# An attention block with a gated branch on one core: first unit's last scores from split operands, second chunk's statistics a step later

## The chip, the cores and the metric

The kernel runs on one core of one Trainium2 chip. The core has five engines that run side by side and meet through semaphores: TensorE (PE, matmuls; PEld is its weight load), VectorE (DVE), ScalarE (ACT), GpSimd (POOL) and SyncE (SP, which here only issues DMAs). Each engine works off its own list of instructions in order. The metric is the device time of one execution in microseconds.

## What is computed

The input x is 2 batches of 1024 tokens with 512 features. All weights are float32.

```python
xn = layernorm(x)
q, k, v = xn @ Wq.T + bq, xn @ Wk.T + bk, xn @ Wv.T + bv      # 32 heads of 16
att = softmax(where(causal, q @ k.T / sqrt(16), -inf))        # per head
s = (att @ v) @ Wo.T + bo
base = xn @ W_base.T + b_base
route_w = top-2 of softmax(xn @ W_gate.T), renormalised       # 8 experts
delta = ((xn @ A.T) * route_w) @ B                            # rank 16 each
out = x + s * silu(base + delta)
```

## The kernel before

The tokens of a batch are two *chunks* of 512 (c = 0, 1). Heads go in four groups of eight (oc = 0 to 3). A *unit* is (batch, group, chunk of the queries); there are 16, and their order is (0,0,0), (0,1,0), (0,0,1), (0,1,1), (0,2,0), (0,3,0), (0,2,1), (0,3,1) and the same for batch 1. A unit is worked off in *steps*: 5 for chunk 0, 13 for chunk 1, so that `plan` has 144 steps, 0 to 143. Units 0, 1 and 2 have the steps 0 to 4, 5 to 9 and 10 to 22; unit 6, (0,2,1), begins at step 46.

A step does this. `scores(n)` multiplies keys and queries of eight heads into two PSUM banks (tiles s, two buffers of a pair's half each; line 1723). ACT takes the exponential of each bank into a tile pt. `values(n - 1)` multiplies the previous step's pt with the values into av (line 1775). `masked(n)` has POOL blank the upper triangle of pt (line 1751). Then `fill(n)` puts other work on PE until the step has its share: projections (`pq`, `pk`, `q`), values and gate products (`p`), the route product (`ph`, of the experts' weights), the output product (`po`). All of it goes through `matmul` (line 258) into PSUM tiles of the tag mm, which has two buffers: each product can begin when the reader of the last but one is through.

Scores come in two forms. The first unit multiplies plain float32: the queries are laid out in two copies, each masked to one head of a pair (`queries(par)` in `first_task`, two DVE operations), and the keys are kf. All other units have *split* operands: a rounded part and the remainder, in tiles of a reduced float format (F32R), so that a score is two cheaper products (`halves`). To make them, ACT copies the rounded part (`split_keys`, `split_queries`), DVE subtracts it, ACT copies the remainder of the queries (`copy_remainder`), and SP moves rows between partitions with DMAs (`place_keys`, `place_queries`, two DMAs each). In the kernel before, the first unit's keys are split too, by the function `apart` at step 4 or later, since unit 2 uses them; its queries are not.

The values of the first chunk are made by a seven-product scheme for 2x2 blocks, which needs sums of weights (t1 to t4, from wv) and of tokens (asum, named s[0] to s[3], from xnT). For the first chunk DVE makes them in `early_values`; the products are named p1, p2, p6, p7, p4 there and p5, p3 in `early_rest`, and `early_add` adds each into v.

The second chunk of batch 0 is normalised in `layernorm_task`: four tiles of statistics (`bn_stats`), the power on POOL (line 282), four normalisations, and then twice: four transposes of 32x32 blocks into the tile sq, one store of sq to memory (scr), four reads of scr into xnT. The tile sq has one buffer (`bufs=1`).

Who comes when is settled when the program is built: `fill` keeps lists (`later`, `urgent`, `splits`, `turns`) and `Task` objects with due times, and a reckoning of when DVE and ACT are free (`Metered`, line 56, through which every DVE and ACT operation is recorded, so that they all show line 56; SP's DMAs show line 72). What it settles is a fixed list for each engine. `room` counts free buffers of a tag. At the end, `test_task` tests that the softmax's sums are in range (tiles ok and fine), and `post_tile` normalises the last unit's tiles (rc_last, olast).

Of the kernel before, what the change touches and what calls it, by code (L numbers as in the profile page):

```python
# [8 lines left out]
F32 = mybir.dt.float32  # L9
# [9 lines left out]
P = 128  # L19
# [12 lines left out]
NEG = -3.0e38  # L32
NF = 2 + 4 * 2 * 4
WARM = 10


Z_LOW, Z_HIGH = 1.0e-20, 1.0e20
# [60 lines left out]
def direct(ctx, tc, sound, x, wq, wk, wv, wo, wb, wa, wg, wB, bq, bk, bv, bo, bb, out):  # L98
# [148 lines left out]
    WAIT = object()  # L247
    PAUSE = object()
    turned_at, now = {}, [0]
    xns, xnTs, kTs, qTs, vs, gs, oTs, kfs = {}, {}, {}, {}, {}, {}, {}, []  # L250

    def mm_tile(name):
        return ps_mm.tile([P, D], F32, tag="mm", name=name)
# [42 lines left out]
    def layernorm_task(b, c):  # L296


        xt = chunk_tile(b, c)
        for i in range(NS):  # L300
            i0 = c * C + i * P
            sp.dma_start(
                out=xt[i * SQ : (i + 1) * SQ],
                in_=x[b, i0 : i0 + P].rearrange("(t r) d -> r t d", r=SQ),
            )
        if b == 0:
            load_rest()
        tiles = [xt[:, t] for t in range(TT)]
        for _ in range(3 if b else 1):
            yield WAIT  # L310
        s = yield from statistics(tiles, True)
        if b:
            yield WAIT
        for t in range(0, TT, 2):
            normalize(tiles[t : t + 2], s[0][:, t : t + 2], s[1][:, t : t + 2])
            yield PAUSE
        if b:
            yield WAIT
        xnT = sb.tile([P, KC, C], F32, tag="xnT", bufs=3, name=f"xnT_{b}_{c}")
        for k0 in range(0, KC, 2):  # L320
            sq = sb.tile([P, 2, NS, TT, SQ], F32, tag="sq", bufs=1, name="sq")
            for t in range(TT):
                yield PAUSE
                ve.transpose(
                    out=sq[:, :, :, t],
                    in_=tiles[t][:, k0 * P : (k0 + 2) * P].rearrange(
                        "p (k q d) -> p k q d", k=2, q=NS
                    ),
                )
            scr = dram.tile([NS, SQ, 2, NS, TT * SQ], F32, tag="scr", name="scr")  # L330

            def store(sq=sq, scr=scr, place=None):
                sp.dma_start(
                    out=scr.rearrange("i d k q m -> (i d) (k q m)"),
                    in_=sq.rearrange("p k q t r -> p (k q t r)"),
                )
                if place:
                    behind.append(place)
                    landed(place, now[0] + 3)

            def place(k0=k0, scr=scr):
                for q in range(NS):
                    sp.dma_start(
                        out=xnT[q * SQ : (q + 1) * SQ, k0 : k0 + 2].rearrange(
                            "d k (i m) -> d k i m", i=NS
                        ),
                        in_=scr[:, :, :, q].rearrange("i d k m -> d k i m"),
                    )
                if k0:
                    turned_at[b, c] = now[0] + int((sp.landing() - sp.now) / 3.4)  # L350

            if not b:
                store()
                place()
                yield WAIT
                continue
            later.append((now[0] + b, lambda s=store, p=place: s(place=p)))
            for _ in range(0 if k0 else 1 + b):
                yield WAIT
        xnTs[b, c] = xnT  # L360

    def first_task():
# [1 line left out]
        xnT = sb.tile([P, KC, C], F32, tag="xnT", bufs=3, name="xnT_0_0")  # L364
        qT = sb.tile([P, 2, C], F32, tag="qT", bufs=2, name="qT_0_0_0")
        kT = sb.tile([P, C], F32, tag="kf", bufs=2, name="kf_0_0_0")
        xnTs[0, 0], qTs[0, 0, 0] = xnT, qT
        kfs.append(kT)
        pq = ps_av.tile([P, C], F32, tag="av", name="pq_first")
        pk = ps_av.tile([P, C], F32, tag="av", name="pk_first")  # L370

# [20 lines left out]
        def queries(par):  # L392
            ve.tensor_scalar(
                qT[:, par], pq, bq_sb[:, 0:1], half[:, par : par + 1], ALU.add, ALU.mult
            )
# [29 lines left out]
        turn(3)  # L425
        room["x"] += 1
        project_first(pk, wqks[0][:, 3 * KC :], 2)
        project_first(pq, wqks[0][:, 2 * KC : 3 * KC], TT - 1)
        queries(0)
        queries(1)  # L430
        ve.stream_shuffle(b_pair, b_sb, PAIRED)
        ve.tensor_tensor(b_less, b_pair[:, 0:KC], b_pair[:, KC:], ALU.subtract)
        project_first(pk, wqks[0][:, 3 * KC :], 3)
        keys(1, TT)
        kTs[0, 0, 0] = sb.tile([P, 2, C], F32R, tag="kT", bufs=4, name="kT_0_0_0")
        low = sb.tile([P, C], F32, tag="rb", bufs=1, name="low_0_0_0")

        def apart():
            ve.stream_shuffle(low, kT, PAIRED)
            split_keys(kTs[0, 0, 0], low, low)  # L440
            later.append((now[0] + 1, lambda: place_keys(kTs[0, 0, 0], low)))

        later.append((0, lambda: pair_up(wqks[1])))
        paired = lambda: pair_up(wqks[0])
        costs[paired], costs[apart] = (1.1, 5), (1.1, 6)
        later.append((3, paired))
        later.append((4, apart))
        yield 8 * MM

    def qk_task(b, oc, c):  # L450
# [72 lines left out]
            both = qT[:, 2 * par : 2 * par + 2].bitcast(F32)  # L523
            sp.dma_start(out=both[1 - par :: 2], in_=both[par::2])

    def last_unit(unit):
        return 1 if unit == units[-1] else 0

    def split(b, oc, c, qf, kf):

        qT, kT = split_tiles(b, oc, c)
        split_keys(kT, kf, kf)

        def queries():
            split_queries(qT, qf)
            room["acc"] += 1
            later.append((now[0] + 1, remainder))

        def remainder():
            copy_remainder(qT)  # L540
            urgent.append((now[0], lambda: place_queries(qT)))

        by = starts[b, oc, c] - last_unit((b, oc, c))
        costs[queries], costs[remainder] = (1.1, by - 4), (0.6, by - 3)
        later.append((now[0] + 1, queries))
        urgent.append((now[0] + 1, lambda: place_keys(kT, kf)))
# [282 lines left out]

    def early_values():

        x0 = xnTs[0, 0]
        at = lambda i, j: x0[:, 2 * j : 2 * j + 2, BK * i : BK * i + BK]
        early_at["w"] = raw = {
            (i, j): wv_sb[:, 2 * i : 2 * i + 2, BK * j : BK * j + BK]
            for i in range(2) for j in range(2)
        }
        t = {  # L840
            n: sb.tile([P, 2, BK], F32, tag="wp", bufs=NWP, name=f"wt{n}") for n in range(1, 5)
        }
        early_sums.update({f"t{n}": t[n] for n in t})
        early_at["s"] = s = [
            sb.tile([P, 2, BK], F32, tag=f"sum{n}", bufs=1, name=f"asum{n}") for n in range(4)
        ]
        vt = value_tile(0, 0)
        for i in range(TT):
            vs[0, i] = vt[:, i]
        hv = heads(vt)  # L850
        early_at["v"] = slot = lambda i, j: hv[:, 2 * i : 2 * i + 2, H // 2 * j : H // 2 * (j + 1), 0:HD]
        s11, s12, s21, s22 = slot(0, 0), slot(0, 1), slot(1, 0), slot(1, 1)
        ve.tensor_tensor(t[1], raw[0, 1], raw[0, 0], ALU.subtract)
        ve.tensor_tensor(s[2], at(0, 0), at(1, 0), ALU.subtract)
        ve.tensor_tensor(s[1], at(1, 1), s[2], ALU.subtract)
        ve.tensor_tensor(t[2], raw[1, 1], t[1], ALU.subtract)
        ve.tensor_tensor(t[3], raw[1, 1], raw[0, 1], ALU.subtract)
        p1 = yield from early_product("p1", at(0, 0), raw[0, 0])
        early_add(s12, p1, early_bias(0))
        ve.tensor_tensor(t[4], raw[1, 0], t[2], ALU.subtract)  # L860
# [621 lines left out]
    for b in range(NB):  # L1482
        for c in range(NC):
            s0 = starts[b, 0, c]
            xn = [("xnT", b, c)]
            if not b and not c:
                room["x"] -= 1
                Task(1, first_task(), 8 * MM, takes={"xnT": 1, "qT": 1, "kT": 1}, uses=xn)
            else:
                Task(  # L1490
                    s0 - (12 if c else 25) if b else -9, layernorm_task(b, c), 0.0, after=s0 - (44 if c == 0 else 30) if b else -9,
                    takes={"x": 1, "xnT": 1}, frees={"x": 1},
                )
# [58 lines left out]
            else:  # L1552
# [2 lines left out]
                n = len(units) - 3  # L1555
                Task(len(plan) - 12, test_task(0, n, 0), 0.0, after=before - 10)
                Task(
                    len(plan) - 1, test_task(n, n + 2, 1), 0.0, after=len(plan) - 3,
                    ready=lambda: sum(len(x) for x in posts.values()) == len(units) - 1,
                )  # L1560
                for t in range(TT - 1):
# [48 lines left out]
    def fill(n):  # L1610
# [52 lines left out]
        enough = lambda more=0.65: late_by(n + 1, begins, more) > 0  # L1663
        calm = lambda more: act.free + more < begins + 0.75
        for x in [x for x in splits if x[0] <= n]:
            if room["qT"] and room["kT"] and (calm(1.1) or n >= starts[x[2]] - 5 - last_unit(x[2])):
                splits.remove(x)
                room["qT"] -= 1
                room["kT"] -= 1
                x[1]()  # L1670
# [38 lines left out]
    def scores(n):  # L1709
# [1 line left out]
        place_urgent(n)  # L1711
        ss = [ps_s.tile([P, 2, C], F32, tag="s", name=f"s{p}") for p in range(2)]
        for m, (par, kt, q0, w, col) in enumerate(pieces):
            first_unit = (b, oc, c) == units[0]
            halves = 1 if first_unit else 2
            keys = kfs[0] if first_unit else kTs[b, oc, kt // TT][:, par]
            q = qTs[b, oc, c]
            for half_ in range(halves):
                for s in range(4):
                    rows = slice(32 * s, 32 * s + 32)  # L1720


                    nc.tensor.matmul(  # L1723
                        ss[s // 2][:, s % 2, col : col + w],
                        lhsT=keys[rows, kt % TT * P : kt % TT * P + P],
                        rhs=q[rows, halves * par + half_, q0 : q0 + w],
                        start=m + half_ == 0,
                        stop=m == len(pieces) - 1 and half_ == halves - 1,
                    )
# [572 lines left out]
```

## Time and profile before

| | us |
|---|---|
| median of 3 timed runs | 544.42 (544.01 to 545.55) |
| the profiled execution, its own time | 544.48 |
| its span in the profile | 542.7 |
| PE busy | 531.8 |
| ACT busy | 351.6 |
| DVE busy | 340.9 |
| PE weight load busy | 282.7 |
| POOL busy | 116.1 |

The granted TensorE clock was 0.998 of full speed over the span. The DMA queue that SP feeds moved 76.78 MB and took 44.7% of the 16 DMA engines' time.

How to read the profile: a timeline line gives start and duration in us from the span's start, the engine, the source line, the operation and the tiles as out<-in, then the number of instructions that were merged into the line, and in brackets how long the engine stood idle before it and what ended that. Matmuls are pipelined and their ends are modelled, so two neighbouring PE groups overlap by some 0.1 to 0.2 us; the distance from start to start is what a group really takes from PE. In the list of waits, the columns are the total in us, how often, and the longest.

### The profile page before, as it was taken

The numbers are of one execution on the slowest core, as the hardware profiler recorded it, in microseconds if no ns is written. First come the engines' busy times: TensorE is split into PE (matmuls) and PEld (weight loads), VectorE is DVE, ScalarE is ACT, GpSimd is POOL, SyncE is SP. The second block draws the span as 40 slices with busy tenths as digits, with TensorE's granted clock in tenths as the row PEclk, the third lists the DMA queues.
The fourth block names the chain that finished last, engine by engine and source line by source line (L and its number), as shares of the span: only waits on it lengthen the run. The fifth ranks groups of instructions, "written<-read, shape, count | busy, mean of one in ns | idle before, by whom it ended". The sixth has DMA issues, their size and how long they took to land.

```text
span 542.7 us, 19905 instructions
## 1 busy us (share of the span) xinstructions
PE 531.8 (98%) x8623; PEld 282.7 (52%) x8623; DVE 340.9 (63%) x706; ACT 351.6 (65%) x387; POOL 116.1 (21%) x249
## 2 busy tenths in 40 slices
PE   7999999999999999999999999999999999999994
PEld 7546445544455554454645554454545564456672
DVE  4863586665585876476369766574277544749843
ACT  2457754776776876757667756657667776877630
POOL 2213401020033422030123320130113330121200
PEclk9999999999999999999999999999999999999999
DMA  7626356356526583813665545640124121653301
GB/s 251 159 93 219 132 165 223 100 187 208 158 100 226 184 265 118 236 43 100 191 164 199 178 142 167 196 153 24 63 95 144 61 85 44 236 170 91 99 29 61
DMA packets 67744, 78.15 MB, mean 144 GB/s; under 512 B 9928, under 2 KB 52944, under 8 KB 67136
## 3 DMA queue, kind: packets, MB, share of 16 engines
q1 hardware_dynamic: 67632, 76.78, 44.7%
q8 instruction: 70, 1.15, 0.9%
q14 instruction: 26, 0.21, 0.1%
q10 hardware_dynamic: 16, 0.00, 0.0%
HBM read 45.34 MB, written 19.37 MB: 119 GB/s over the span
## 4 chain that ended last, share of the span: by engine, by line
PE 94%; DVE 3%; DMA 2%; issue 0%; SPq 0%; DVEq 0%
PE av L1775 26%; PE p L258 25%; PE s L1723 18%; PE q L258 14%; PE ph L258 3%; PE po L258 2%; PE pk L258 1%; PE pq L258 1%; DMA wqk<-in_wq_dram 1%; PE pq_first L388 1%; PE h L258 1%; DMA kept<-w_gate 1%; DVE g L56 1%; PE pk_first L388 0%; PE pt_o L258 0%; DVE wt L56 0%
## 5 line engine op out<-in xcount | busy, mean ns | idle before, releaser
L56 ACT ACTIVATE pt<-s 128x1024 f32<-128x1024 f32 x288 | 290.5, 1024 | 151.0 <-PE s L1723 147.0
L1751 POOL TENSOR_SCALAR_AFFINE_SELECT pt<-pt 128x256 f32<-128x256 f32 (+1 forms) x224 | 107.4, 494 | 399.5 <-ACT pt L56 398.9
L1775 PE MATMUL av<-pt,v 128*32 128x512 f32 (+3 forms) x1680 | 154.3, 467 | 0.2 <-DVE oT L56 0.2
L1723 PE MATMUL s<-qT,kT 32*128 32x512 f32 (+3 forms) x1616 | 106.7, 363 | 0.0
L1723 PEld LDWEIGHTS s<-qT,kT 32*128 32x128 f32 x1616 | 61.2, 183 | 56.5 <-issue 34.6
L1775 PEld LDWEIGHTS av<-pt,v 128*32 128x32 f32 x1680 | 40.9, 108 | 53.6 <-issue 38.3
L258 PE MATMUL p<-wt,asum 128*32 128x256 f32 x960 | 58.4, 379 | 0.4 <-DVE v L56 0.4
L258 PE MATMUL q<-asum,wqk 128*32 128x256 f32 x832 | 51.1, 379 | 0.0
L258 PEld LDWEIGHTS p<-wt,asum 128*32 128x32 f32 x960 | 30.9, 110 | 30.0 <-issue 12.6
L258 PE MATMUL q<-xnT,wqk 128*32 128x256 f32 x624 | 39.5, 379 | 0.0
L258 PEld LDWEIGHTS q<-asum,wqk 128*32 128x32 f32 x832 | 26.8, 110 | 23.7 <-issue 6.6
L258 PEld LDWEIGHTS q<-xnT,wqk 128*32 128x32 f32 x624 | 20.2, 110 | 18.5 <-issue 6.6
L56 DVE SCALAR_TENSOR_TENSOR kf<-q,kf 128x256 f32<-128x256 f32 x39 | 16.5, 422 | 20.6 <-PE q L258 20.0
L56 DVE TENSOR_TENSOR g<-p,g 128x512 f32<-128x512 f32 x20 | 13.8, 689 | 23.5 <-PE p L258 23.4
L258 PE MATMUL p<-w,xnT 128*32 128x256 f32 x448 | 27.6, 379 | 0.0
L56 DVE TENSOR_TENSOR v<-p,v 128x512 f32<-128x512 f32 x22 | 14.9, 683 | 13.4 <-PE p L258 13.3
L258 PE MATMUL p<-w,asum 128*32 128x256 f32 x320 | 21.0, 379 | 0.0
L258 PEld LDWEIGHTS p<-w,xnT 128*32 128x32 f32 x448 | 14.8, 110 | 10.6 <-issue 3.3
L258 PEld LDWEIGHTS ph<-wag_sb,xnT 128*32 128x32 f32 x512 | 15.2, 110 | 3.9 <-issue 3.3
L56 DVE TENSOR_TENSOR x<-p,x 128x512 f32<-128x512 f32 x15 | 10.3, 685 | 10.4 <-PE p L258 10.4
L258 PE MATMUL ph<-wag_sb,xnT 128*32 128x136 f32 x512 | 16.6, 279 | 0.0
L56 ACT ACTIVATE qT<-qf 128x1024 fp32r<-128x1024 f32 x15 | 15.8, 1054 | 0.1
(156 smaller groups left out, 563.6 us busy)
## 6 DMA issues: line engine op xcount, KB each, us to landing
wt<-kept SPq DMA_DIRECT2D x36, 256.0 KB
qT<-qT SPq DMA_DIRECT2D x30, 256.0 KB
x<-in_x_dram SPq DMA_DIRECT2D x16, 256.0 KB
kept<-wqk SPq DMA_DIRECT2D x16, 256.0 KB
wqk<-kept SPq DMA_DIRECT2D x4, 1024.0 KB
kT<-kf SPq DMA_DIRECT2D x30, 128.0 KB
scr<-sq SPq DMA_DIRECT2D x6, 512.0 KB
xnT<-scr SPq DMA_DIRECT2D x24, 128.0 KB
```

The costliest lines, as they stand in the source:

```text
L56: return getattr(self.engine, name)(*args, **named)
L258: nc.tensor.matmul(o[j : j + 32], lhsT=lhsT[:, j : j + 32] if len(lhsT.shape) == 2 else lhsT[:, j // 32], rhs=rhs, start=start, stop=stop,)
L388: nc.tensor.matmul(ps[:, cols], lhsT=w[:, k, :], rhs=xnT[:, k, cols], start=k == 0, stop=k == KC - 1)
L1723: nc.tensor.matmul(ss[s // 2][:, s % 2, col : col + w], lhsT=keys[rows, kt % TT * P : kt % TT * P + P], rhs=q[rows, halves * par + half_, ...
L1751: nc.gpsimd.affine_select(out=d, in_=d, compare_op=ALU.is_ge, fill=0.0, base=0, pattern=[[0, d.shape[1]], [1, P]], channel_multiplier=-1,)
L1775: nc.tensor.matmul(avs_now[par][32 * s : 32 * s + 32, q0 : q0 + w], lhsT=vs[b, kt][:, h * VS - HD * par : h * VS - HD * par + HP], rhs=pt[ ...
```

## The change

Five things are done.

1. `early_begin`, called in `first_task` before the last part of the query projection, makes three weight sums (t1, t2, t3) and one token sum (s[2]); they were made in `early_values`, behind the queries. It calls the vector engine directly, so the planner's reckoning doesn't count them.
2. The first unit's queries are written by ACT as a whole too (qf). `apart` now comes in step 0 and splits keys and queries: two shuffles, two ACT copies, two differences, then the keys' DMAs and, by `remainder`, the copy of the remainder and the queries' DMAs. Steps below `SPLIT_FROM` (3) use the plain operands (`whole_first`), steps 3 and 4 the split ones; the plain queries' buffer is given back at step 2.
3. The second chunk's `layernorm_task` waits two turns instead of one ahead of its statistics (batch 0).
4. `last_unit` becomes `sooner`, which is 1 for unit 6 also: its split may be a step earlier.
5. The second range test may begin at step `len(plan) - 4` (140) instead of 141.

In the lists that result, PE has the same order of work as before, with the split form in steps 3 and 4. On DVE, the second chunk's normalisations and all eight transposes come behind the difference of unit 1's keys and ahead of the additions of p5; before, the normalisations and the first four transposes came ahead of p4's addition, and the second four behind unit 1's keys. On SP, the first unit's four split DMAs come ahead of unit 1's, and the first store and reads of scr, which came ahead of unit 1's queries and keys, come behind them; the first unit's keys came behind den before. On POOL, the power comes behind step 2's masks. Around step 45, unit 6's query split stands one step earlier on ACT, DVE and SP.

```diff
+SPLIT_FROM = 3
...
-        for _ in range(3 if b else 1):
+        for _ in range(3 if b else 2):
             yield WAIT
...
-        xnTs[0, 0], qTs[0, 0, 0] = xnT, qT
-        kfs.append(kT)
+        xnTs[0, 0] = xnT
+        whole_first.extend((qT, kT))
...
         project_first(pk, wqks[0][:, 3 * KC :], 2)
+        early_begin()
         project_first(pq, wqks[0][:, 2 * KC : 3 * KC], TT - 1)
         queries(0)
         queries(1)
+        qf = sb.tile([P, C], F32, tag="qf", bufs=2, name="qf_0_0_0")
+        act.activation(qf, pq, AF.Identity, bias=bq_sb[:, 0:1])
...
-        kTs[0, 0, 0] = sb.tile([P, 2, C], F32R, tag="kT", bufs=4, name="kT_0_0_0")
+        q2, k2 = split_tiles(0, 0, 0)
         low = sb.tile([P, C], F32, tag="rb", bufs=1, name="low_0_0_0")
+        turns.append((SPLIT_FROM - 1, lambda: room.update(qT=room["qT"] + 1)))
 
         def apart():
+            qs = sb.tile([P, C], F32, tag="qf", bufs=2, name="qs_0_0_0")
             ve.stream_shuffle(low, kT, PAIRED)
-            split_keys(kTs[0, 0, 0], low, low)
-            later.append((now[0] + 1, lambda: place_keys(kTs[0, 0, 0], low)))
+            ve.stream_shuffle(qs, qf, PAIRED)
+            split_keys(k2, low, low)
+            split_queries(q2, qs)
+            later.append((now[0] + 1, lambda: place_keys(k2, low)))
+            later.append((now[0] + 1, remainder))
+
+        def remainder():
+            copy_remainder(q2)
+            urgent.append((now[0], lambda: place_queries(q2)))
 
         later.append((0, lambda: pair_up(wqks[1])))
         paired = lambda: pair_up(wqks[0])
-        costs[paired], costs[apart] = (1.1, 5), (1.1, 6)
+        costs[paired] = 1.1, 5
+        later.append((0, apart))
         later.append((3, paired))
-        later.append((4, apart))
...
-    def last_unit(unit):
-        return 1 if unit == units[-1] else 0
+    def sooner(unit):
+        return 1 if unit in (units[6], units[-1]) else 0
...
-    def early_values():
+    def early_begin():
...
+        nc.vector.tensor_tensor(t[1], raw[0, 1], raw[0, 0], ALU.subtract)
+        nc.vector.tensor_tensor(t[2], raw[1, 1], t[1], ALU.subtract)
+        nc.vector.tensor_tensor(t[3], raw[1, 1], raw[0, 1], ALU.subtract)
+        nc.vector.tensor_tensor(s[2], at(0, 0), at(1, 0), ALU.subtract)
+
+    def early_values():
+
+        at, raw, t, s = early_at["x"], early_at["w"], early_at["t"], early_at["s"]
...
-        ve.tensor_tensor(t[1], raw[0, 1], raw[0, 0], ALU.subtract)
-        ve.tensor_tensor(s[2], at(0, 0), at(1, 0), ALU.subtract)
         ve.tensor_tensor(s[1], at(1, 1), s[2], ALU.subtract)
-        ve.tensor_tensor(t[2], raw[1, 1], t[1], ALU.subtract)
-        ve.tensor_tensor(t[3], raw[1, 1], raw[0, 1], ALU.subtract)
...
-                Task(1, first_task(), 8 * MM, takes={"xnT": 1, "qT": 1, "kT": 1}, uses=xn)
+                Task(1, first_task(), 8 * MM, takes={"xnT": 1, "qT": 2, "kT": 1}, uses=xn)
...
-                    len(plan) - 1, test_task(n, n + 2, 1), 0.0, after=len(plan) - 3,
+                    len(plan) - 1, test_task(n, n + 2, 1), 0.0, after=len(plan) - 4,
...
-            first_unit = (b, oc, c) == units[0]
-            halves = 1 if first_unit else 2
-            keys = kfs[0] if first_unit else kTs[b, oc, kt // TT][:, par]
-            q = qTs[b, oc, c]
+            whole = n < SPLIT_FROM
+            halves = 1 if whole else 2
+            keys = whole_first[1] if whole else kTs[b, oc, kt // TT][:, par]
+            q = whole_first[0] if whole else qTs[b, oc, c]
```

More of the change, by code (lines that the diff above doesn't have):

```diff
@@ L249, in direct @@
     turned_at, now = {}, [0]
-    xns, xnTs, kTs, qTs, vs, gs, oTs, kfs = {}, {}, {}, {}, {}, {}, {}, []
+    xns, xnTs, kTs, qTs, vs, gs, oTs, whole_first = {}, {}, {}, {}, {}, {}, {}, []
     def mm_tile(name):
@@ L541, in remainder @@
             urgent.append((now[0], lambda: place_queries(qT)))
-        by = starts[b, oc, c] - last_unit((b, oc, c))
+        by = starts[b, oc, c] - sooner((b, oc, c))
         costs[queries], costs[remainder] = (1.1, by - 4), (0.6, by - 3)
@@ L828, in direct @@
     early_sums, early_at, early_tasks = {}, {}, []
-    def early_values():
+    def early_begin():
         x0 = xnTs[0, 0]
-        at = lambda i, j: x0[:, 2 * j : 2 * j + 2, BK * i : BK * i + BK]
+        early_at["x"] = at = lambda i, j: x0[:, 2 * j : 2 * j + 2, BK * i : BK * i + BK]
         early_at["w"] = raw = {
@@ L839, in early_values @@
         }
-        t = {
+        early_at["t"] = t = {
             n: sb.tile([P, 2, BK], F32, tag="wp", bufs=NWP, name=f"wt{n}") for n in range(1, 5)
@@ L1665, in fill @@
         for x in [x for x in splits if x[0] <= n]:
-            if room["qT"] and room["kT"] and (calm(1.1) or n >= starts[x[2]] - 5 - last_unit(x[2])):
+            if room["qT"] and room["kT"] and (calm(1.1) or n >= starts[x[2]] - 5 - sooner(x[2])):
                 splits.remove(x)
```

## The prediction, made before the changed kernel was run

> **What bounds the kernel now.** I read the page's busy line and chain first. TensorE (PE) is busy for 98% of the span and carries 94% of the chain that ended last, so a change counts only by the idle time or the matmul time that it takes from PE or gives to it.
>
> ```profile
> PE 531.8 (98%) x8623; PEld 282.7 (52%) x8623; DVE 340.9 (63%) x706; ACT 351.6 (65%) x387; POOL 116.1 (21%) x249
> ...
> PE 94%; DVE 3%; DMA 2%; issue 0%; SPq 0%; DVEq 0%
> ```
>
> Then the list of what PE waited for. After the start it names three waits that this change can touch or must not lengthen.
>
> ```profile
> PE p L258 <- DVE v L56: 0.4, 1, 0.4
> PE pt_o L258 <- DVE olast L56: 0.4, 1, 0.4
> PE av L1775 <- DVE oT L56: 0.2, 1, 0.2
> ```
>
> Last the timeline of 12 to 62 us and of the tail. Columns: start, duration, engine, line, operation.
>
> ```profile
> 27.90 1.15 PE L1723 MATMUL s<-qT,kf 32*128 32x384 f32 x16
> ...
> 30.85 1.41 DVE L56 STREAM_TRANSPOSE sq<-x 128x256 f32<-128x256 f32 x4
> ...
> 32.29 0.33 SPq L72 DMA_DIRECT2D scr<-sq  x1
> ...
> 36.07 2.65 SPq L72 DMA_DIRECT2D xnT<-scr  x4
> ...
> 38.14 1.15 PE L1723 MATMUL s<-qT,kf 32*128 32x384 f32 x16
> ...
> 40.08 0.69 DVE L56 TENSOR_TENSOR kf<-kf,kT 128x512 f32<-128x512 f32 x1 [2.74 <-ACT kT L56]
> ...
> 40.69 1.42 DVE L56 STREAM_TRANSPOSE sq<-x 128x256 f32<-128x256 f32 x4
> ...
> 42.08 1.29 DVE L56 TENSOR_TENSOR v<-p,v 128x512 f32<-128x512 f32 x2
> ...
> 42.13 0.40 SPq L72 DMA_DIRECT2D scr<-sq  x1
> ...
> 45.00 2.59 SPq L72 DMA_DIRECT2D xnT<-scr  x4
> ...
> 47.30 2.27 PE L258 MATMUL ph<-wag_sb,xnT 128*32 128x136 f32 x72
> ...
> 53.64 0.80 PE L1723 MATMUL s<-qT,kT 32*128 32x384 f32 x16
> ...
> 521.22 0.19 DVE L56 TENSOR_SCALAR ok<-dens 128x64 f32<-128x64 f32 x1
> ...
> 521.84 0.17 DVE L56 RECIPROCAL rc_last<-pt_o 128x4 f32<-128x4 f32 x1
> ...
> 522.67 0.43 PE L258 MATMUL pt_o<-ident,olast 128*32 128x128 f32 x8 [0.37 <-DVE olast L56]
> ```
>
> To see here: the second chunk's two groups of transposes stand 9.8 us apart (30.85 and 40.69), with the store that empties sq (32.29) between them and landed by 36.07, when the reads of scr go out. The adds that free the bank of p5 (42.08) end 3.9 us before the route product ph (47.30), which is the next to use that bank.
>
> **The change part by part.** I take PE by its issue slots: the distance between the starts of neighbouring groups.
>
> *Value sums in front of the first queries.* Four sums (t1, t2, t3, s2) of 0.68 each are 2.72. DVE was idle for 3.19 before the queries at 15.78 (12.59 to 15.78), and s2 needs the last copy of xnT, which ends at 14.44. So they are covered if wv is there by 13.06; the first loads' traffic falls off at 13.0 to 13.3 and has a trickle to 14.0. I take 0, with 0.9 as the upper end. What is won: before, the add of p1 came at 21.06 behind the sums, and p6 started at 21.79 although PE's slots were through at 21.17. Now the add of p1 can start at 19.7. Gain 0.62.
>
> *Splitting the first unit early.* New on DVE: a shuffle (0.76) and a difference (0.68); a shuffle and a difference of the keys come forward from 48.33 and 54.18. New on ACT: qf (0.69), qT (1.06), the copy of the remainder (0.63); the keys' 1.06 comes forward from 53.09. SP gets two DMAs more (qT) and two sooner (kT); they stand on SP ahead of everything for unit 1, go out at about 28 and are needed at step 3, at 37.25: the two projections between (6.86) hide them, and only a landing of over 8 us would stall step 3. ACT and DVE are in order, so step 1's exponentials go behind the split: p2's add ends at 22.0, low 23.2, kT 23.2 to 24.2, qT to 25.2, pt to 27.15 instead of 25.6. Step 2's second bank is asked for at 27.28, so this is hidden by 0.13; each tenth beyond would be paid. Along the slots PE then ends pk at 37.13 (before 38.02): 0.89 gained, the 0.62 and small gaps at 22 to 28.
>
> *Steps 3 and 4 cheaper.* The f32 step took 1.07 (38.14 to 39.21), a split one of the same columns 0.73 (53.64 to 54.37). Step 4: 1.08 (41.94 to 43.02) against 0.68 (63.10 to 63.78). Nominal gain 0.74. Step 4 must wait for step 3's exponentials, which stand behind unit 1's key split on ACT and end at about 41.1, while PE is there at 40.7: some 0.4 comes back at once. PE would reach ph at 46.06 instead of 47.30.
>
> *Statistics a step later: the term that decides.* In the changed kernel's instruction list DVE now has, in this order: difference of unit 1's keys, four normalisations, four transposes, four transposes, the two adds of p5, the add of p3. The tile sq has one buffer, so the first of the second four waits for the store of the first four to complete. The two groups, 9.8 us apart before, are now neighbours, and the adds of p5 are queued behind that wait; ph, waiting for DVE, needs p5's bank. Chain: pk ends 37.13; the keys' difference starts 2.06 later as before (38.02 to 40.08), 39.19; normalisations from 39.80, 1.93 for four (28.92 to 30.85), 41.73; transposes 1.41; store; landing; transposes 1.39 to the adds (40.69 to 42.08); adds 1.29 and 0.05 to PE.
>
> Landing of the store: the four rows in which scr's reads wait for little else give 3.78 (32.29 to 36.07), 2.87 (42.13 to 45.00), 3.91 (247.97 to 251.88), 3.55 (263.09 to 266.64). I take 3.5, ends 2.87 and 3.91.
>
> [...] The normalisations now fall on step 2's and step 3's masks on POOL (about 40 to 42). The row nearest: two normalisations with one mask started in them took 1.20 (165.47), without one 0.99 (168.00), so 0.2 per mask, 0.5 for two or three. [...] I take the row's 0.5 and keep 0 and 1.6 as ends.
>
> So: 41.73 + 0.5 + 1.41 + 0.03 + 3.5 + 1.39 + 1.34 = 49.9 for ph, against 47.30 before: **2.6 lost**. PE waits there from 46.06, 3.8 in all, so everything gained above it (0.89 on PE's side of pk excepted, which is in the chain) is swallowed. Low end: 41.73 + 1.41 + 0.03 + 2.87 + 1.39 + 1.34 = 48.8, 1.5 lost.
>
> Behind it SP is late too: first reads of scr from 47.2, second store 49.85, second reads 53.35 to 55.95, then the four stores of wt, two loads, den, and unit 2's queries at about 66. PE needs xnT's second half at 56.11 + 2.6 = 58.7, 2.8 after the last issue, and unit 2's queries at 66.51 + 2.6 = 69.1, some 2 after theirs. I take 0 for both, with 1.5 as the upper end. After that everything hangs on PE's pace again (SP waits for other engines nearly throughout), so the shift stays.
>
> *Unit 6's queries a step sooner.* ACT's 1.05 moves from 183.91 to about 181.14, behind the tanh ending there, and delays the exponentials at 182.00 by 0.2; their banks are asked for at 184.55 and 184.7, when they are done (183.2 and 184.2). The wait for sq's store at 181.99 stays behind it. SP's two DMAs were issued at 189.17 for 194.97. Nothing on PE; I take 0.
>
> *Range test in step 140.* Three operations of 0.62 together stood between 521.22 and 521.84, ahead of the reciprocal that PE's 522.67 waits for. Now they lie in DVE's pause from 514.74 to 515.88. olast ends 0.62 sooner; PE's av ends its slots at 522.12. Gain 0.55, and PE runs from there to the end without a longer gap, so it is kept.
>
> **Sum**, against the profiled execution of 544.48 (span 542.7 and 1.8 around it): + 2.6 - 0.55 = + 2.05, 546.5. The median of the timed runs, 544.42, is the same to 0.06; I predict 546.5.
>
> **The rivals.**
> *Stall hidden, gains kept (faster).* For it: PE bound, 0.62 + 0.74 + 0.55 nominal. Its place is ph; it decides from the point where p5's adds are done by 46.1. Against it: the first transposes cannot end before 43.1, and 1.39 + 1.34 are still to come, so even a store landing at once gives 45.9. It needs DVE to run the adds ahead of the waiting transposes, which a list in order does not do, or PE to have other bank space. Time: 544.48 - 1.24 - 0.55 = 542.7, and 542.3 if step 4's wait is shorter too. Chance 0.12.
> *A short stall.* Landing 2.87 and no blocking by masks: + 1.5 - 0.55 = 545.4, within the bound. For it the row at 42.13; against it the other three stores. Chance 0.23.
> *More waits behind it.* xnT's second half or unit 2's queries late, or wv late in front, or full blocking by masks: 1 to 1.5 more, 547.5 to 548. For it SP's queue, now some 8 us behind at 55 against 2.6 for PE; against it the traffic, which leaves DMA at 35 to 60% there. Chance 0.15.
> The main case, 545.9 to 547.2, has 0.50.
>
> **How the numbers follow.** 0.3% of 544.42 is 1.63, about what a measurement of this kernel can tell from no change: faster below 542.8, slower above 546.05. Main case and more waits give slower 0.62, allowing that a little of the main case lies below 546.05; the short stall and that part, same 0.27; faster 0.11. For 8 in 10 the range goes from 544.3 (leaving out the hidden stall and a bit between) to 548.0.
>
> **What would show it.** p6 starting at about 21.2 behind p2 without a wait on v; steps 3 and 4 in slots of 0.7; two transpose groups on DVE with 3 to 4 us between them waiting for scr's store; a new PE wait, ph on DVE v, of 3 to 4 us at 46 to 50; no wait of pt_o on olast at the end. Wrong if PE does not wait at ph, if step 3 waits for the split keys' DMA, or if a wait of more than 1 us appears elsewhere.

## The result, and the profile after

| | before | after |
|---|---|---|
| median of 12 runs, us | 544.42 (544.01 to 545.79) | 547.20 (545.81 to 548.16) |
| the profiled execution, its own time | 544.48 | 548.16 |
| its span | 542.7 | 546.4 |

The ratio is 1.0046, with a 95% interval from 1.0035 to 1.0058: slower, by 2.8 us between the medians, where 2.05 had been forecast.

The twelve times after are not one heap. Six lie from 545.81 to 546.58 (mean 546.29) and six from 547.82 to 548.16 (mean 548.00), with nothing between. The mean granted clock is 0.996 to 0.999 in each of the first six and 0.992 to 0.995 in each of the second. The profiled execution is of the second kind, and the median of 547.20 lies between the two groups, where no execution does.

The page of the kernel after, busy line and granted clock in 40 slices:

```profile
PE 534.4 (98%) x8623; PEld 285.1 (52%) x8623; DVE 342.7 (63%) x709; ACT 353.4 (65%) x390; POOL 116.0 (21%) x249
...
PEclk9998999999999999999999999999999999999998
```

PE is busy for 2.6 us more than before (534.4 against 531.8), although steps 3 and 4 use a cheaper form. The 8 in the fourth slice is the place, 41 to 55 us (the 8 at the end lies behind PE's last work). In the list of what PE waited for, the three waits shown of before are gone, and one is new:

```profile
PE ph L259 <- DVE v L57: 2.9, 1, 2.9
```

The timeline of the kernel after (start, duration, engine, line, operation):

```profile
16.19 1.14 PE L1740 MATMUL s<-qT,kf 32*128 32x512 f32 x8
...
20.74 0.61 PE L259 MATMUL p<-wt,asum 128*32 128x256 f32 x8
...
37.05 0.80 PE L1740 MATMUL s<-qT,kT 32*128 32x384 f32 x16
...
38.99 0.69 DVE L57 TENSOR_TENSOR kf<-kf,kT 128x512 f32<-128x512 f32 x1 [2.74 <-ACT kT L57]
39.60 2.18 DVE L57 TENSOR_SCALAR x<-x,mv,rstd 128x512 f32<-128x512 f32 x4
...
39.94 2.10 POOL L1768 TENSOR_SCALAR_AFFINE_SELECT pt<-pt 128x256 f32<-128x256 f32 x4 [7.50 <-ACT pt L57]
...
40.50 1.08 PE L1740 MATMUL s<-qT,kT 32*128 32x256 f32 x16
...
41.70 1.41 DVE L57 STREAM_TRANSPOSE sq<-x 128x256 f32<-128x256 f32 x4
...
43.14 0.34 SPq L73 DMA_DIRECT2D scr<-sq  x1
...
44.80 0.74 PE L1740 MATMUL s<-qT,kT 32*128 32x512 f32 x8
...
46.70 2.65 SPq L73 DMA_DIRECT2D xnT<-scr  x4
46.78 1.42 DVE L57 STREAM_TRANSPOSE sq<-x 128x256 f32<-128x256 f32 x4 [3.67 <-DMA scr<-sq]
48.12 1.85 DVE L57 TENSOR_TENSOR v<-p,v 128x512 f32<-128x512 f32 x3
49.43 3.10 PE L259 MATMUL ph<-wag_sb,xnT 128*32 128x136 f32 x72 [2.89 <-DVE v L57]
...
525.96 0.40 PE L259 MATMUL pt_o<-ident,olast 128*32 128x128 f32 x8
```

The order on DVE is the one that the forecast followed: normalisations, transposes, 3.67 of waiting for the store of scr, transposes, adds, and then ph. The tail's wait on olast is gone. Not in the forecast is the length of ph: 3.10 for the same 72 matmuls that took 2.27 before. The table of windows shows why. Its columns are the window, its length, PE's busy time with matmuls, the granted clock, the DMA share and GB/s:

```profile
47.00:49.00 2.00, 0.00 (x0) 1.00 0.24 68
49.00:51.00 2.00, 1.57 (x52) 0.94 0.79 204
51.00:52.00 1.00, 1.00 (x24) 0.50 0.99 362
52.00:54.00 2.00, 2.00 (x24) 0.50 0.22 80
54.00:56.00 2.00, 2.00 (x52) 0.96 0.45 131
```

Soon after PE's 2.89 us of idle time the clock falls to half, for 3.4 us.

Step 0 of the kernel before, from which the times below are counted:

```profile
16.64 1.14 PE L1723 MATMUL s<-qT,kf 32*128 32x512 f32 x8
```

Where the 3.68 us of the two profiled executions come from: step 0 starts at 16.19 instead of 16.64 (-0.45). This is not put down to the change: in the other profiles with the same first part it starts anywhere from 16.03 to 16.53, and without that part at 16.00 (part 3 alone). From step 0 to ph it is 33.24 instead of 30.66 (+2.58). From ph to pq, 6.94 (49.43 to 56.37) instead of 5.37 (+1.57): the half clock. From there to the scores at 519.58 (515.74 before), +0.14. From these to pt_o at 525.96, 6.38 instead of 6.93 (-0.55). From pt_o to the end, +0.4, of which 0.29 lies in PE's last products and weighted values (532.12 to 536.30, before 528.86 to 532.75); what causes it is open.

### The profile page after: what moved, and what is told of

Read it like the earlier page. It is cut to its first block, busy times and chain, and to the rows that moved or that the text cites. A ratio compares the mean times of both kernels' runs of the same rounds, so it can differ in the third digit from the quotient of the medians.

```text
span 546.4 us, 19914 instructions
## 1 busy us (share of the span) xinstructions
PE 534.4 (98%) x8623; PEld 285.1 (52%) x8623; DVE 342.7 (63%) x709; ACT 353.4 (65%) x390; POOL 116.0 (21%) x249
## 4 chain that ended last, share of the span: by engine, by line
PE 95%; DVE 2%; DMA 1%; ACT 0%; issue 0%; POOL 0%; POOLq 0%; DVEq 0%
PE av L1792 26%; PE p L259 25%; PE s L1740 18%; PE q L259 14%; PE ph L259 3%; PE po L259 2%; PE pk L259 1%; PE pq L259 1%; PE warm L214 1%; PE pq_first L389 1%; PE h L259 1%; PE pk_first L389 1%; DMA scr<-sq 1%; DVE sq L57 1%; PE pt_o L259 0%; DVE x L57 0%
## 5 line engine op out<-in xcount | busy, mean ns | idle before, releaser
L1740 PE MATMUL s<-qT,kT 32*128 32x512 f32 (+3 forms) x1648 | 109.0, 363 | 0.0
L1740 PEld LDWEIGHTS s<-qT,kT 32*128 32x128 f32 x1648 | 62.7, 184 | 58.1 <-issue 34.4
L1792 PEld LDWEIGHTS av<-pt,v 128*32 128x32 f32 x1680 | 41.1, 109 | 54.2 <-issue 38.6
L57 DVE TENSOR_TENSOR g<-p,bb_sb 128x512 f32<-128x512 f32 x8 | 5.5, 690 | 17.2 <-PE p L259 17.1
```

What stands on the lines that cost most here:

```text
L57: return getattr(self.engine, name)(*args, **named)
L1740: nc.tensor.matmul(ss[s // 2][:, s % 2, col : col + w], lhsT=keys[rows, kt % TT * P : kt % TT * P + P], rhs=q[rows, halves * par + half_, ...
L1792: nc.tensor.matmul(avs_now[par][32 * s : 32 * s + 32, q0 : q0 + w], lhsT=vs[b, kt][:, h * VS - HD * par : h * VS - HD * par + HP], rhs=pt[ ...
```

## The experiments

**Is the one buffer of sq the cause?** Second tile for the second four transposes, in space that lies free until 111.9.

```diff
+            if b == 0 and k0:
+                sq = sb.tile([P, TT, D], F32, tag="g", bufs=1, name="sq2")[:, 0:2].rearrange(
+                    "p k (q t r) -> p k q t r", q=NS, t=TT
+                )
+            else:
                 sq = sb.tile([P, 2, NS, TT, SQ], F32, tag="sq", bufs=1, name="sq")
```

> Edit: the changed kernel, but the second four transposes write a tile of their own (in the space of g, which is first used at 111.9). Theory A (the one buffer of sq is the cause of ph's stall): the transposes follow one another at 41.7 and 43.1, the adds of p5 end at about 45.9, before PE is there (46.5); ph waits for nothing, the 2.9 us of idle PE and the clock that falls after it are gone, every execution is near 543.5 (546.4, the lower group of the changed kernel's times, less 2.9), and the times no longer fall into two groups. Theory B (DVE is late by its other work, normalisations and masks): ph still waits by 1 us or more, and the time stays at 546 or above.

Measured: 547.86 (546.89 to 549.29), 1.0056 [1.0035, 1.0076]. Both theories missed it. In the trace ph starts at 46.70 and waits for nothing, as A says, and yet nothing is won: even the six executions at a clock of 0.997 have a median of 547.5 (the other four are at 0.994 and took 548.58 to 549.29). PE's list of waits and SP's timeline of this kernel:

```profile
PE pq L259 <- DMA xnT<-scr: 2.8, 1, 2.8
...
PE pq L259 <- ACT hl L57: 0.9, 1, 0.9
```

```profile
43.48 0.34 SPq L73 DMA_DIRECT2D scr<-sq  x1
47.05 2.65 SPq L73 DMA_DIRECT2D xnT<-scr  x4
49.80 1.45 SPq L73 DMA_DIRECT2D scr<-sq  x1
54.22 2.54 SPq L73 DMA_DIRECT2D xnT<-scr  x4
```

The second transposes were done at 44.75, but their store went out at 49.80: it stands on SP behind the first reads, which wait for the first store. Then the second reads wait for the second store. So the second half of xnT lands at 59.6, where the kernel before had it in time for its use at 56.11, and pq pays 2.8 instead of ph. (The 0.9 is put down to ACT; the first difference of tokens on DVE, at 53.02, shows that the first half of xnT landed then, just ahead of pq's 53.15.) The wait at ph hid this one: in the kernel after, the same half landed at 58.29 and is used at 59.80 (pq's 58.94 and a third of its 24 matmuls, 0.86).

**The order on SP.** The same, with both stores issued ahead of the first reads:

```diff
                 store()
-                place()
+                if k0:
+                    places[0]()
+                    place()
+                places.append(place)
```

> Edit: the second tile for the second four transposes as above, and SP issues both stores of scr ahead of the first reads. Theory E (what part 3 costs is the way of the second chunk's transposed tokens over SP: store, 3.6 of waiting, reads, store, 4.4 of waiting, reads; the one buffer only decides whether PE pays at ph or at pq): the first reads go out at 47.1 as before, the second at 49.7 instead of 54.2, the second half of xnT lands at 55.5 instead of 59.6; pq waits 0.9 for the first half and nothing for the second; 547.5 less 2.8: 544.4 to 545.0. Rival (the second half is held up by something else, say the traffic): it still lands after 58 and the time stays above 546.5.

Measured: 543.31 (542.82 to 544.11), 0.9982 [0.9974, 0.9991]: faster than before, and 3.9 below the kernel after. SP's timeline, and PE's pq:

```profile
43.31 1.78 SPq L73 DMA_DIRECT2D scr<-sq  x2
46.66 6.00 SPq L73 DMA_DIRECT2D xnT<-scr  x8
...
53.92 3.67 PE L259 MATMUL pq<-xnT,wqk 128*32 128x512 f32 x32
```

All reads are out by 52.66 instead of 56.76, and PE's list of waits names nothing over 0.2 but a 1.4 at the very start, which every kernel here has. Theory E holds for the second half: half of pq's 32 matmuls need it, these begin at about 55.6 (halfway from 53.92 on), and PE does not wait. The time is 1.1 to 1.7 below the theory's, as the 0.9 for the first half is gone too. The planner had put all 32 matmuls of pq behind step 6 here, from 53.92, so that they ask later; that part of the gain is the order on PE, not SP's, and its share of the time is not shown.

**Part 3 undone**, the rest of the change kept.

```diff
-        for _ in range(3 if b else 2):
+        for _ in range(3 if b else 1):
```

> Edit: the changed kernel with part 3 undone (one turn of waiting ahead of the second chunk's statistics, as before). Theory A: no wait of ph, the rest of the change keeps what it won: 542.7 (544.42 less 0.55 at the tail, and 1.2 less in front), no two groups. Rival (the other parts lose as well, the early split above all): 544 or more, with waits on PE between 22 and 47 that the kernel before does not have.

Measured: 548.42 (546.56 to 549.28), 1.0066 [1.0043, 1.0088]; the clock was at or under 0.993 in six of eight runs. The rival is right. DVE and PE of this kernel:

```profile
24.71 0.69 DVE L57 TENSOR_TENSOR qT<-qs,qT 128x512 fp32r<-128x512 f32 x1 [0.25 <-ACT qT L57]
25.32 0.68 DVE L57 BATCH_NORM_STATS2 st<-x 128x6 f32<-128x512 f32 x1
...
28.71 1.48 DVE L57 TENSOR_TENSOR v<-p,v 128x512 f32<-128x512 f32 x2
...
29.45 1.00 PE L259 MATMUL p<-wt,xnT 128*32 128x256 f32 x8 [3.04 <-DVE v L57]
```

The early split (till 25.3) pushes the statistics (till 28.7) in front of the adds of p6, whose bank p4 needs. The kernel with parts 1 and 5 alone (below) has neither the split nor this wait. In this program parts 2 and 3 are one thing: with the split in step 0, the statistics cannot stay in step 1.

**Part 3 alone**, put into the kernel before.

```diff
-        for _ in range(3 if b else 1):
+        for _ in range(3 if b else 2):
```

> Edit: the kernel before with part 3 alone (two turns of waiting ahead of the second chunk's statistics). Theory A with the working of the forecast: difference of unit 1's keys done at 40.8, normalisations 42.8, first transposes 44.3, store landed 47.8, second transposes 49.2, adds 50.6: ph at 50.6 instead of 47.3, 3.3 lost: 547.7, and 549.3 in the executions in which the clock falls afterwards, the idle time being 3.3 long. Rival B: ph waits by less than 2 us and the time is under 546.5.

Measured: 549.03 (547.31 to 550.15), 1.0072 [1.0046, 1.0097]; five of six runs at a clock of 0.992 to 0.995. In the profiled one (550.15), ph starts 33.51 after step 0 (16.00 to 49.51), 2.85 later than before, for which 3.3 was expected; the store landed in 3.2 (43.57 to 46.78), not 3.5. Then the clock halves (49.8 to 53.2), and unit 2's first score waits 1.0 for its queries' DMA. So part 3 without anything else costs all that the change costs, and more.

**Parts 1 and 5 alone**, in the kernel before: `early_begin` ahead of the last part of the queries, and `after=len(plan) - 4`.

> Edit: the kernel before with parts 1 and 5 alone (four sums in front of the queries; second range test in step 140). Theory (each of the two wins what the forecast says, on its own): p6 starts 0.6 sooner and keeps it, olast ends 0.6 sooner: 544.42 less 0.62 less 0.55: 543.3. Rival (what is won in front is lost at the next wait before step 5): 543.9.

Measured: 543.08 (542.57 to 544.69), 0.9980 [0.9974, 0.9987]: 1.0 below the 544.12 of its own runs of before. The theory holds. It is level with the repaired version of the whole change (543.31), without the split.

This kernel also shows what steps 3 and 4 win and lose. Its profiled execution and that of the kernel after both start step 0 at 16.19, and are equal to 0.01 until step 3. PE's scores in it, and POOL's masks of step 3:

```profile
37.04 1.15 PE L1728 MATMUL s<-qT,kf 32*128 32x384 f32 x16
...
39.93 1.68 POOL L1756 TENSOR_SCALAR_AFFINE_SELECT pt<-pt 128x256 f32<-128x256 f32 x4 [9.03 <-ACT pt L56]
...
40.85 1.15 PE L1728 MATMUL s<-qT,kf 32*128 32x256 f32 x16
...
44.65 0.74 PE L1728 MATMUL s<-qT,kT 32*128 32x512 f32 x8
...
46.21 2.27 PE L258 MATMUL ph<-wag_sb,xnT 128*32 128x136 f32 x72
```

After: 37.05, 40.50, 44.80. Step 3 wins 0.36 (3.45 instead of 3.81) and step 4 loses 0.50 (4.30 instead of 3.80). Step 5 is the same: 1.56 from its start to ph's here, and 1.55 in the second-tile kernel, where ph doesn't wait either (45.15 to 46.70). So PE is 0.15 behind at ph. In the kernel after, PE's weight loads show the waits in step 4:

```profile
40.84 0.54 PEld L1740 LDWEIGHTS s<-qT,kT 32*128 32x128 f32 x14 [0.15 <-ACT pt L57]
42.09 0.24 PEld L1792 LDWEIGHTS av<-pt,v 128*32 128x32 f32 x8 [0.40 <-POOL pt L1768]
```

The second is not the price of the split. The exponentials come at the same time in both kernels (38.87 and 38.86), and so do the masks (39.94 and 39.93), but in the kernel after the masks take 2.10 instead of 1.68, with part 3's four normalisations on DVE running over them, and end 0.43 later. With part 3 undone, where no normalisation lies there, they take 1.68 again, and step 4 takes 3.90. (With part 3 alone, in plain float32, they take 2.10, and step 4 takes 3.95 instead of 3.80.)

```profile
44.74 1.68 POOL L1768 TENSOR_SCALAR_AFFINE_SELECT pt<-pt 128x256 f32<-128x256 f32 x4 [9.03 <-ACT pt L57]
...
45.28 1.10 PE L1740 MATMUL s<-qT,kT 32*128 32x256 f32 x16
...
49.18 0.74 PE L1740 MATMUL s<-qT,kT 32*128 32x512 f32 x8
```

So the split form alone wins 0.36 in step 3 and loses 0.10 in step 4; part 3 takes another 0.40 there.

**The clock: fill the idle time.** In the kernel after, p3 is computed twice into the same tile, so that PE works in most of the gap.

```diff
+        for _ in range(times - 1):
+            for i in range(2):
+                for kc in range(2):
+                    matmul(ps[:, i * BK : i * BK + BK], lhsT=a[:, kc, i * P : i * P + P], ...)
```

> Edit: the changed kernel, but the product p3 is computed twice into the same tile (the second overwrites the first), so that PE works for some 2 us of its 2.9 us of idle time ahead of ph; the result is the same. Theory C (the idle time makes the clock fall afterwards, and this is the second group of times): ph still starts at 49.4 to 49.6, the granted clock stays at 1.00 behind it, and all executions lie at 546.0 to 546.6; none near 548. Rival D (the two groups come from the start of the run, or from the traffic of DMAs at that place, not from idle PE): the times still fall into two groups 1.6 apart.

Measured: median 546.20; nine of eleven runs from 545.84 to 546.58, and two at 547.30 and 548.51, whose mean clock is 0.997 like that of the others. In the trace ph waits 0.96 and starts at 49.06, and the clock is at 1.00 from 45 to 55. PE does 1.7 us more work than in the kernel after, and the median is 1.0 lower. That is theory C, but for the two stragglers: they are not low in clock, so they are not its slow group, and what made them is open.

**Two more doses of idle time.** Half of p3 twice:

> Edit: the changed kernel with half of the product p3 computed twice, some 0.9 us more of work on PE ahead of ph, so that its idle time there is 2.0 instead of 2.9. Theory C (the share of executions in which the clock falls rises with the idle time: 1.0 gave none in the record of clocks, 2.9 half): ph at 49.4 as before, most executions at 545.9 to 546.6, at most a third near 548. Rival (any wait here over 1 us is enough, or chance of the day): half or more near 548.

and, the other way, the second four transposes twice, ahead of the adds:

```diff
+            if b == 0 and k0:
+                for t in range(TT):
+                    nc.vector.transpose(...)
```

> Edit: the changed kernel with the second four transposes done twice (the same values again), 1.4 us more of DVE work ahead of the adds of p5, so that PE is idle for 4.3 in front of ph instead of 2.9. Theory C: the clock falls in every execution and there is one group of times: 546.4 + 1.4 + 1.6 = 549.4 or a little more, as the later xnT adds nothing to a PE that is late by as much. Rival D: still two groups, at 547.8 and 549.4.

Measured: with half of p3, idle 1.93, five runs from 545.75 to 547.32 (median 546.45), all at clocks of 0.997 or 0.998. With the transposes doubled, idle 4.03, five runs from 548.70 to 549.76 (median 549.25), all at 0.990 to 0.995, in one group. Its windows:

```profile
47.00:49.00 2.00, 0.00 (x0) 1.00 0.36 101
49.00:51.00 2.00, 0.57 (x12) 0.75 0.90 233
51.00:52.00 1.00, 1.00 (x24) 0.50 0.90 352
52.00:53.00 1.00, 1.00 (x27) 0.50 0.07 29
53.00:54.00 1.00, 1.00 (x32) 0.79 0.00 0
54.00:55.00 1.00, 1.00 (x20) 1.00 0.44 131
```

Together, by PE's longest wait after the start in the profiled execution, the executions with a mean clock of 0.995 or less:

| kernel | wait, us | of all executions |
|---|---|---|
| p3 twice | 0.96 | 0 of 11 |
| half of p3 twice | 1.93 | 0 of 5 |
| part 3 alone | 2.54 | 5 of 6 |
| second tile (at pq) | 2.79 | 4 of 10 |
| the kernel after | 2.89 | 6 of 12 |
| part 3 undone (at p4) | 3.04 | 7 of 8 |
| transposes doubled | 4.03 | 5 of 5 |

In each kernel that has both kinds, those are the slowest executions. Theory C holds in that no clock fell at 1.93 or less and every one did at 4.03, and the windows show the fall behind waits at two places of the program, ph and p4, which speaks against rival D. In between the share does not rise evenly (5 of 6 at 2.54, 4 of 10 at 2.79), and the wait is known for one execution of each kernel only. (The mean clock alone proves little: single runs of the kernel before had 0.995 at 544.07. It counts here with the two groups of times and the windows.)

**Part 4 undone**, in the version with both stores first.

```diff
-        return 1 if unit in (units[6], units[-1]) else 0
+        return 1 if unit in (units[-1],) else 0
```

> Edit: the version with two tiles and both stores first (543.31), with part 4 undone: unit 6's query split a step later, as in the kernel before. The forecast put part 4 at nothing: 543.3 within 0.3. Rival: the split is late for unit 6 now that PE is sooner there: 543.8 or more, with a wait of a score on DMA qT near 195.

Measured: 543.06 (542.84 to 543.25), 0.9977 [0.9968, 0.9987], against 0.9982 [0.9974, 0.9991] with it. No difference, and no wait of a score.

## Why the prediction was right, and where it was not

The forecast was 546.5 and slower; it came to 547.20. The half of the executions without the fall of the clock has a median of 546.38, 1.96 above before where the sum said 2.05. The mechanism is the forecast's; that the size fits so closely is in part luck, as two of its errors cancel (the deciding term, below).

- *Sums in front of the queries, 0.62 gained:* right. From step 0 to step 1 it is 5.10 (16.19 to 21.29) instead of 5.72, and p6 has no wait.
- *Early split hidden, pk 0.89 sooner:* hidden, yes. But step 3 is only 0.64 sooner counted from step 0 (20.86 against 21.50), and the kernel with parts 1 and 5 alone has the same. The small gaps that the sum had added to the 0.62 were not won.
- *Steps 3 and 4, 0.74 nominal and 0.4 given back:* this term was mis-sized. Step 3 won its 0.36; step 4, which was to win 0.40 and give some 0.4 back, lost 0.50. The forecast had the scores wait for step 3's exponentials, but put nothing for the weighted values that follow them in step 4 and wait for POOL's masks of step 3: it reckoned what these masks do to part 3's normalisations, and not what the normalisations do to the masks. It did not show in the time, as PE was ready for ph only 0.5 sooner than before (44.80 and 1.55 is 46.35, 30.16 from step 0 against 30.66) instead of 1.24, and waited there anyway.
- *The deciding term, ph 2.6 late:* right, 2.58 from step 0, but two parts cancel. The keys' difference, where the chain begins, came 0.25 later from step 0 than forecast (38.99 - 16.19 = 22.80 instead of 22.55). The normalisations took 2.10 from start to start (39.60 to 41.70), 0.33 less than the forecast's 1.93 and 0.5. Landing was 3.56 (43.14 to 46.70) against 3.5. The forecast's 1.93 had a mask over it already (30.24, its row 28.92 to 30.85); with part 3 undone, four normalisations without a mask take 1.82 (30.84 to 32.66). So four masks cost DVE 0.28, and cost POOL 0.42 (2.10 instead of 1.68): both engines were slowed, and neither stood still for the whole of the other's operations. No run shows the 1.6 that the forecast kept as an end, about the masks' own time (1.68), nor the full blocking by masks of one of its rivals.
- *SP's backlog, 0 with 1.5 as the upper end:* right for this kernel: the second half of xnT landed at 58.29, 1.5 ahead of its use, which ph's wait had put off, as the forecast reckoned (56.11 + 2.6). What it did not carry over is that with ph's wait away the same backlog costs 2.8. With part 3 alone, unit 2's queries cost 1.0.
- *The faster rival, 542.7 if ph's wait is hidden:* priced wrongly. Its condition was met by the second tile, and the time was 547.86. It left out that SP's list is in order too, so that store, reads, store and reads come one after another (issued at 43.48, 47.05, 49.80 and 54.22 there). To get the gain, both places have to be mended: 543.31.
- *Unit 6 and the range test:* right: 0, and 0.55 (6.93 to 6.38).
- *What the sum did not have:* the half clock after a long wait, 1.6 us in half of the executions. It is the 0.7 by which the median passed the forecast; as just six of twelve fell, the median came out in the middle between the groups (546.38 and 547.98), and one more or fewer would have moved it to an edge of one of them. The rival with "more waits behind it" named 547.5 to 548 for other reasons; it is not what happened.

## What to carry to other kernels

When a stall is found, ask what it covers: give each later consumer of the delayed data its own time of need before saying what removing the first wait is worth. Where data goes out and comes back through one in-order queue, issue all stores ahead of the first reads that wait for one (547.86 to 543.31 here, with PE's order changed too). Of the kernels here whose profile has a wait of PE of 2.5 to 4 us, 27 of 41 executions had the low mean clock (0.995 or less), and half a clock for 3.4 us is 1.7 us of work: count with that beside a stall of this length. When work is moved on one engine, ask also whom it slows beside it: the normalisations cost the masks 0.42, and PE waited for the masks.

## What the runs showed of the hardware

The slow phase had one length and no fixed place in the four profiles that show it. Worked out from their windows, the clock is at 0.50 for 3.4 us each time: from about 50.8 to 54.2 in the kernel after, 29.6 to 33.0 with part 3 undone, 49.8 to 53.2 with part 3 alone, and 50.0 to 53.4 with four transposes more. It begins 1.3 us after PE works again in the kernel after (49.43), 0.2 and 0.3 after in the two kernels with part 3 undone and alone (29.45 and 49.51), and 0.4 before in the one with four transposes more (50.43). What sets the length and the place is not shown. PE's gaps ahead of it were 2.89, 3.04, 2.54 and 4.03, while a gap of 2.79 (second tile) had no slow phase behind it in its profile, though four of that kernel's ten executions have the low clock. Behind gaps of 0.96 and 1.93 none of 16 executions has a mean clock under 0.997, and no profile here has a gap between 1.93 and 2.54. A low mean clock was also seen in a kernel whose profile has no such wait: of 25 executions of the kernel before in one session, two had 0.993 and took 548.0 and 548.2. They were not profiled, so what PE waited for in them is open.
